# A graph attention layer whose steps leave their per-product queues for one timetable over three groups

## The chip, the cores and the metric

The kernel runs on one core of a Trainium2 chip. The metric is device time in microseconds (us) of one execution. The times given are medians of several runs; the profile is of one further execution, whose span is given beside them. Engine names are those of the profile: PE (matmul) with PEld (its weight loads), DVE, ACT, POOL, and SP, which issues the DMAs.

## What is computed

The input `x` has 128 graphs of 128 nodes with 768 features; `adj` has one 128 x 128 matrix per graph. There are 12 heads of 64 features.

```python
h = jnp.maximum(_layernorm(x, axis=-1), 0.0)
q, k, v = (_split_heads(h @ W + b) for W, b in ((Wq, bq), (Wk, bk), (Wv, bv)))
scores = jnp.einsum('bhqd,bhkd->bhqk', q, k) / jnp.sqrt(HD) + beta * adj[:, None]
scores = jnp.where(adj[:, None] > 0, scores, -9e15)
out = jnp.einsum('bhqk,bhkd->bhqd', softmax(scores), v)
x = x + out.transpose(0, 2, 1, 3).reshape(B, N, D)
```

All is in float32.

## The kernel before

**Groups and slices.** Four graphs make a group; there are 32 groups, 0 to 31. For each group three slices of the projections are computed: `qk0` (Q and K of heads 0 to 5), `v`, and `qk1` (Q and K of heads 6 to 11). Group 0 does them by ordinary blocked matmuls (`plain_slice`, L834); in that stage the weights' blocks are also prepared. Groups 1 to 31 do each slice as a fast matrix multiplication, 15 block products instead of the ordinary count (`PRODUCTS`, L66): each product multiplies one sum of activation blocks (`S..`, or a block `A..` itself) by one prepared sum of weight blocks (`T..`). So a group has 45 products, and this document numbers them as slots 0 to 44: 0 to 14 `qk0`, 15 to 29 `v`, 30 to 44 `qk1`. A product is itself made of seven zones (L556), each two matmuls of 128 rows, 64 stationary columns and 128 moving columns (L561); a float32 matmul leaves two records, so a product leaves 28.

**Chains and PSUM.** The fifteen products belong to four chains, a to d (third entry of a row in `PRODUCTS`). A chain adds up in one pair of PSUM banks; four such pairs exist (L160), handed out in turn (`take`, `give`). After each product the chain's running sum is evicted into the Q, K or V block that uses it (L567 to L585): the first time into a fresh "home" by ACT (the opening, L579 and L581; for V by DVE and ACT, L575 and L576), later by DVE, which adds or subtracts (L585). The chain's next product can start only when the eviction has read the bank. A pair is also taken by each step of scores (L631) and by each attend (L687), so these share the four pairs with the chains. Homes are seven plus one added after group 0 (L527, L1076), handed out in turn too.

**Blocks that are streamed.** Of the 45 weight blocks 11 are resident (`RESIDENT`, L116, by their place in the sequence of a group); the other 34, of 448 KB each, are loaded for each group into a ring of five buffers (`load_T`, L336). A load is issued on SP right behind the product that frees the buffer.

**The other steps of a group.** When the last eviction of a home is done, it is decoded on POOL, sometimes on DVE (L595): four or five elementwise operations that undo the zones. Scores of a pair of heads follow (L640), then the mask on DVE (L648), which writes e and frees the pair, and exp on ACT (L650). An attend is woven into the matmuls of one product (`turn`, L522); ACT then takes the result from the bank (the drain, L707 and L709), DVE makes reciprocals (L668), ACT divides (L680), DVE adds x (L725), and SP sends the result (L728). For the next group x is loaded (L191), normalized on ACT (L452), transposed by DVE (L473), completed by POOL (`inner`, L483 to L485), and summed by DVE into the `S` blocks (L478). For the group after that, rows of x are loaded (L415) and their sums and sums of squares taken on ACT (L423 to L425). The bias of a group is loaded from adj on SP (L492), transposed by DVE (L501), squared in place on ACT (L502), masked and added up by DVE (L504, L506).

**What sets the order.** The program is written in the order in which each engine executes it, each engine's queue being in order. `run` (L822) issues the matmuls of a product, then `behind_product` (L812): masks waiting, then the steps that a table gives for this slot (`todo`, filled from L1082 on), then drains, then steps put off by a count of slots (`later`, L512); then the product's evictions, then `trail` (exp, divide), then the slot's "post" steps. So an eviction always stands behind its slot's sums and transposes, and decodes, divisions and additions come a fixed number of slots behind what they follow. The order of the products within a slice is given by hand (L109 to L114).

Of the kernel before, what the change touches and what calls it, by code (L numbers as in the profile page):

```python
# [10 lines left out]
F32 = mybir.dt.float32  # L11
# [97 lines left out]
ZORDER = (1, 0, 3, 5, 2, 7, 10, 6, 11, 13, 4, 9, 14, 8, 12)  # L109
QORDER = (4, 0, 1, 8, 2, 3, 5, 6, 7, 10, 9, 11, 13, 12, 14)  # L110
LORDER = (1, 4, 0, 8, 5, 2, 10, 3, 6, 7, 13, 9, 11, 12, 14)
# [8 lines left out]
LAG = {("v", 8): 4, ("v", 12): 4, ("qk1", 11): 4}  # L120
ZONES = (5, 1, 2, 3, 4, 0, 6)
LEFT = (6, 2, 1, 4, 3, 5, 0)
# [5 lines left out]
def direct(ctx, tc, x, adj, wq, bq, wk, bk, wv, bv, beta, out, bad):  # L128
# [141 lines left out]
    def prepare(sl):  # L270

        def home(name):
            n = [i for i, p in enumerate(PRODUCTS) if p[1] == name][0]
            if (sl, n) in resident:
                return resident[sl, n]
            made_in[0] += sl != "qk1"
            if sl != "qk1" and made_in[0] % 8 in (2, 5, 7):
                t = work.tile([P, 2, W], F32, tag="e", name=f"prep_{sl}_{n}", bufs=3)
                return t.rearrange("p i w -> p (i w)")[:, 0:7 * P].rearrange("p (z n) -> p z n", n=P)
            return work.tile([P, 7, P], F32, tag="T", name=f"prep_{sl}_{n}", bufs=RING)  # L280
# [46 lines left out]
    def order_of(G, sl):  # L327
        if G == 1 and sl == "qk0":
            return ZORDER
        return LORDER if G == NG - 1 and sl == "qk1" else ORDER[sl]  # L330
# [22 lines left out]
    bqk = const.tile([P, 3, NC], F32, name="bqk")  # L353
# [51 lines left out]
    rows = {}  # L405
# [21 lines left out]
    def row_moments(G, first=5, then=8):  # L427

        ve = stat.tile([P, GRP], F32, tag="verow", name=f"verow_{G}", bufs=1)
        nc.vector.tensor_scalar(ve, rows[G][:, 2], 1.0 / D, EPS, op0=ALU.mult, op1=ALU.add)  # L430
        mean = rows[G][:, 1]
        t = stat.tile([P, 2, GRP], F32, tag="row2", name=f"row2_{G}", bufs=1)

        def powers():
            nc.gpsimd.tensor_tensor(t[:, 0], ve, nhalf.to_broadcast([P, GRP]), ALU.pow)
            nc.gpsimd.tensor_tensor(t[:, 1], mean, t[:, 0], ALU.mult)

        later(powers, 2)
        to = stat.tile([P, NB, 2, GRP], F32, tag="block2", name=f"block2_{G}", bufs=1)
        turned = dram.tile([SQ, NB, 2 * GRP], F32, name=f"turned_{G}")  # L440
        later(lambda: nc.sync.dma_start(turned.rearrange("i b s -> b i s"), t.rearrange("p s g -> p (s g)")), first)
        later(lambda: nc.sync.dma_start(to.rearrange("p b s g -> p (b s g)"),
                                        turned.rearrange("i b s -> i (b s)")[None].to_broadcast([NB, SQ, NB * 2 * GRP])), then)
        for g in range(GRP):
            for b in range(NB):
                rstd[G, g * NB + b], shift[G, g * NB + b] = to[:, b, 0, g:g + 1], to[:, b, 1, g:g + 1]

# [14 lines left out]
    def home_A(G, name):  # L462
        if (G, name) in wide:
            return A[G, name]
        t = wide[G, name] = work.tile([P, 2 * GRP, P], F32, tag=name, name=f"{name}_{G}", bufs=1 + (name[1] == "0"))
        full[G, name] = t[:, 0:7]
        A[G, name] = t[:, GRP:2 * GRP].rearrange("p (c g) n -> p c (g n)", c=2)
# [12 lines left out]
    def inner(G, name):  # L480
        t = wide[G, name]
        e = nc.gpsimd
        e.tensor_tensor(t[:, 0:2], t[:, 7:8].to_broadcast([P, 2, P]), t[:, 5:7], ALU.subtract)  # L483
        e.tensor_tensor(t[:, 2], t[:, 6], t[:, 0], ALU.subtract)
        e.tensor_tensor(t[:, 3], t[:, 4], t[:, 2], ALU.subtract)  # L485
# [9 lines left out]
    turned = {}  # L495

    def bias_steps(G):

        raw = turned.pop((G, "raw")).rearrange("p g b j -> p g (b j)")
        t = biasT[G] = work.tile([P, GRP, N], F32, tag="biasT", name=f"biasT_{G}", bufs=2)  # L500
        nc.vector.transpose(t, raw)  # L501
        trailing.append(lambda: nc.scalar.activation(raw, raw, AF.Square, scale=beta_s, accum_out=seen[:, NG + G:NG + G + 1]))  # L502
        yield
        nc.vector.tensor_scalar(raw, t, 0.0, MASKED, op0=ALU.is_le, op1=ALU.mult)  # L504
        yield
        nc.vector.scalar_tensor_tensor(t, t, beta_c, raw, op0=ALU.mult, op1=ALU.add)  # L506
# [20 lines left out]
    homes = deque(const.tile([P, 7, P], F32, name=f"home{i}") for i in range(7))  # L527
# [17 lines left out]
    def product_z(G, sl, n):  # L545
# [6 lines left out]
        p = banks[chain].rearrange("p i (z w) -> p (i z) w", w=P)  # L552
# [13 lines left out]
        yield  # L566
        for (r, j), sign in uses:  # L567
            key = (G, sl, r, j)
            op = ALU.add if sign > 0 else ALU.subtract
            if key not in qk:  # L570
                left[key] = sum(k == (r, j) for q in PRODUCTS for k, _ in q[3])
                t = qk[key] = home_qk(*key, zones=True)
                if sl == "v":
                    bias = bv_b[:, j * 2 * P:(j + 1) * 2 * P].rearrange("p (i n) -> p i n", i=2)
                    nc.vector.tensor_tensor(t[:, 5:7], bias, p[:, 5:7], op)  # L575
                    nc.scalar.activation(t[:, 0:5], p[:, 0:5], AF.Copy, scale=float(sign))  # L576
                else:
                    oc = j + 3 * int(sl[2])
                    nc.scalar.activation(t[:, 0:5], p[:, 0:5], AF.Copy, scale=float(sign))  # L579
                    for at, of in ((5, 0), (6, 2)):  # L580
                        nc.scalar.activation(t[:, at], p[:, at], AF.Identity, bias=bqk[:, of, oc:oc + 1],  # L581
                                             scale=float(sign))
            else:
                t = qk[key]
                nc.vector.tensor_tensor(t, t, p[:, 0:7], op)  # L585
            left[key] -= 1
            if not left[key]:
                last = order_of(G, sl) is LORDER
# [704 lines left out]
```

## Time and profile before

| | |
|---|---|
| median of 3 runs | 2685.24 us (2683.63 to 2687.36) |
| span of the profiled execution | 2683.5 us |
| busy: PE, PEld, DVE, POOL, ACT | 2654.5, 2564.6, 2179.1, 2073.5, 1750.2 us |
| group 0 (span's start to 124.2) | 124.2 us |
| group 1 | 83.9 us |
| groups 2 to 30 | 2371.7 us |
| group 31 to its last product's end | 88.5 us |
| end behind the last product | 15.2 us |
| DMA | 721.71 MB, mean 269 GB/s |

A row of a timeline gives the start, the time taken, the engine, the line, the operation, and output and input tiles with the count; what stands in brackets is the idle time before it and what ended it. A row of waits gives engine, tile and line that waited, and for what, then the total in us, how often, and the longest. A row of the windows gives a stretch, its length, the busy time and the count of each of PE, PEld, DVE, ACT and POOL, then the granted clock of PE, the DMA engines' share, and GB/s. Matmuls overlap, so a matmul's own time is longer than its distance to the next; distances from start to start tell PE's pace.

### The profile page before, as it was taken

The page shows a single profiled execution, that of the slowest core. Times are in us where ns is not written, and L with a number is a line of the kernel's source. Part 1 is how long each engine was busy: PE and PEld are TensorE (multiplying, and loading weights), DVE is VectorE, ACT ScalarE, POOL GpSimd, SP SyncE. Part 2 cuts the span into 40 slices and gives each one's busy share as a digit, 9 for nine tenths or more (in the row PEclk, how much of TensorE's full clock was granted, in tenths as well). Part 3 has the DMA queues.
Part 4 walks back from the last instruction along what each step waited for, and adds up shares of the span by engine and source line. Part 5 has one row for each costly group of instructions (what it writes and reads, how often), then busy time and mean ns, then how long its engine had stood idle before and what let it go on. Part 6 is the DMA issues. An engine that isn't in the chain of part 4 may idle for free.

```text
span 2683.5 us, 121478 instructions
## 1 busy us (share of the span) xinstructions
PE 2654.5 (99%) x52029; PEld 2564.6 (96%) x52029; DVE 2179.1 (81%) x2701; ACT 1750.2 (65%) x4608; POOL 2073.5 (77%) x3043
## 2 busy tenths in 40 slices
PE   9999999999999999999999999999999999999998
PEld 7799999999999999999999999999999999999997
DVE  6878888878888788888788877788877888877885
ACT  1567766676666677666766666776667676667654
POOL 5877778877778777788777787777887777877774
PEclk9999999999999999999999999999999999999999
DMA  9889888989889898889899889988898998898875
GB/s 232 286 253 281 280 270 274 280 264 284 275 267 279 262 285 270 273 276 279 265 281 279 270 269 278 279 274 276 269 278 265 274 284 270 272 274 274 258 239 162
DMA packets 530341, 721.71 MB, mean 269 GB/s; under 512 B 105980, under 2 KB 374024, under 8 KB 529800
## 3 DMA queue, kind: packets, MB, share of 16 engines
q1 hardware_dynamic: 528640, 713.12, 86.5%
q8 instruction: 411, 6.73, 1.0%
q10 hardware_dynamic: 1160, 0.79, 0.2%
q14 instruction: 130, 1.06, 0.1%
HBM read 647.73 MB, written 66.05 MB: 266 GB/s over the span
## 4 chain that ended last, share of the span: by engine, by line
PE 48%; POOL 27%; ACT 12%; issue 5%; DMA 5%; DVE 3%; SPq 1%; ACTq 0%; POOLq 0%; DVEq 0%
PE pair L561 36%; PE pair L697 4%; POOL v L618 4%; PE pair L857 3%; PE pair L640 3%; POOL v L617 3%; POOL home L616 3%; POOL A L483 3%; ACT x L452 3%; ACT e L650 2%; POOL home L603 2%; POOL home L605 2%; ACT home L579 2%; ACT home L581 2%; POOL v L614 2%
## 5 line engine op out<-in xcount | busy, mean ns | idle before, releaser
L585 DVE TENSOR_TENSOR home<-home,pair 128x896 f32<-128x896 f32 x810 | 861.1, 1076 | 276.2 <-PE pair L561 223.8
L561 PE MATMUL pair<-sbig,T_qk 128*64 128x128 f32 x13020 | 832.8, 273 | 2.9 <-DMA T_qk<-kept_qk 2.0
L561 PEld LDWEIGHTS pair<-sbig,T_qk 128*64 128x64 f32 x13020 | 707.8, 137 | 12.7 <-issue 6.9
L561 PE MATMUL pair<-A,T_qk 128*64 128x128 f32 x6944 | 465.3, 273 | 0.4 <-ACT e L709 0.4
L680 ACT ACTIVATE e<-e,sm 128x64 f32<-128x64 f32 x1512 | 383.0, 348 | 109.2 <-DVE sm L668 109.2
L603 POOL TENSOR_TENSOR home<-home 128x256 f32<-128x256 f32 x298 | 246.6, 828 | 267.8 <-DVE home L585 260.1
L561 PE MATMUL pair<-T_v,sbig 128*64 128x128 f32 x6944 | 417.4, 274 | 1.5 <-issue 1.5
L697 PE MATMUL pair<-v,e 128*64 128x65 f32 x6048 | 400.8, 221 | 5.6 <-DVE e L648 5.5
L579 ACT ACTIVATE home<-pair 128x640 f32<-128x640 f32 x325 | 231.7, 713 | 261.4 <-PE pair L561 200.9
L561 PEld LDWEIGHTS pair<-T_v,sbig 128*64 128x64 f32 x6944 | 381.5, 137 | 14.9 <-issue 13.1
L561 PEld LDWEIGHTS pair<-A,T_qk 128*64 128x64 f32 x6944 | 376.9, 137 | 5.4 <-ACT e L709 5.0
L697 PEld LDWEIGHTS pair<-v,e 128*64 128x64 f32 x6048 | 355.5, 137 | 15.6 <-DVE e L648 12.6
L561 PE MATMUL pair<-sbig,res_qk 128*64 128x128 f32 x4340 | 288.3, 273 | 0.0
L606 POOL TENSOR_TENSOR home<-home 128x256 f32<-128x256 f32 x298 | 239.7, 804 | 23.4
L604 POOL TENSOR_TENSOR home<-home 128x256 f32<-128x256 f32 x298 | 229.8, 771 | 23.4
L561 PEld LDWEIGHTS pair<-sbig,res_qk 128*64 128x64 f32 x4340 | 234.5, 137 | 5.3 <-issue 5.3
L707 ACT ACTIVATE sm<-pair,tiny 128x8 f32<-128x8 f32 x189 | 49.6, 262 | 283.2 <-PE pair L697 283.1
L452 ACT ACTIVATE x<-x,block 128x192 f32<-128x192 f32 x480 | 232.9, 557 | 0.0
L605 POOL TENSOR_TENSOR home<-home 128x128 f32<-128x128 f32 x298 | 212.6, 713 | 23.4
L648 DVE SCALAR_TENSOR_TENSOR e<-pair,biasT 128x1024 f32<-128x1024 f32 x189 | 225.1, 1217 | 4.7 <-PE pair L640 4.7
L650 ACT ACTIVATE e<-e 128x1024 f32<-128x1024 f32 x189 | 193.8, 1065 | 49.3 <-DVE e L648 46.1
L483 POOL TENSOR_TENSOR A<-A 128x256 f32<-128x256 f32 x186 | 168.6, 906 | 56.5 <-DVE A L473 56.5
(201 smaller groups left out, 4602.4 us busy)
## 6 DMA issues: line engine op xcount, KB each, us to landing
T_qk<-kept_qk SPq DMA_DIRECT2D x713, 448.0 KB, 4.9
T_v<-kept_v SPq DMA_DIRECT2D x341, 448.0 KB, 4.7
xo<-in_x_dram SPq DMA_DIRECT2D x189, 256.0 KB, 4.2
out_dram<-xo SPq DMA_DIRECT2D x189, 256.0 KB, 5.9
x<-in_x_dram SPq DMA_DIRECT2D x248, 192.0 KB, 6.8
sbig<-in_x_dram SPq DMA_DIRECT2D x116, 384.0 KB, 6.2
kept_qk<-prep_qk SPq DMA_DIRECT2D x23, 448.0 KB, 3.0
adj<-in_adj_dram SPq DMA_DIRECT2D x128, 64.0 KB, 3.9
```

Of the source, the lines that this page charges most:

```text
L452: nc.scalar.activation(t, t, AF.Relu, bias=shift[G, n], scale=rstd[G, n])
L483: e.tensor_tensor(t[:, 0:2], t[:, 7:8].to_broadcast([P, 2, P]), t[:, 5:7], ALU.subtract)
L561: nc.tensor.matmul(p[q:q + HD, at, :], lhs[:, q:q + HD], rhs, start=(first and at % 4 == 0), stop=True, skip_group_check=True)
L579: nc.scalar.activation(t[:, 0:5], p[:, 0:5], AF.Copy, scale=float(sign))
L585: nc.vector.tensor_tensor(t, t, p[:, 0:7], op)
L603: e.tensor_tensor(t[:, 1:4:2], t[:, 1:4:2], twice(5), ALU.add)
L604: e.tensor_tensor(t[:, 2:5:2], t[:, 2:5:2], twice(1), ALU.add)
L605: e.tensor_tensor(t[:, 4], t[:, 4], t[:, 6], ALU.add)
L606: e.tensor_tensor(t[:, 0:7:6], t[:, 0:7:6], twice(2), ALU.add)
L650: trailing.append(lambda: nc.scalar.activation(e, e, AF.Exp, scale=1.0 / ISCALE))
L680: nc.scalar.activation(o[:, r, b, 0:HD], pa[:, r, b, 0:HD], AF.Copy, scale=t[:, 1, r, b:b + 1])
L697: nc.tensor.matmul(pa[q:q + HD, 2 * g + i, :], k[:, q:q + HD], vt[G, "v", r, h // 4][:, 4 * g + h % 4, :], start=True, stop=True, skip_gro ...
```

## The change

**Steps become single actions with a time of their own.** The eviction is split from the product; mask, exp, drain, reciprocals, division, addition, sending, and the parts of the bias and of the row moments are functions that can be placed one by one. Each gets a time in slots (45 to a group) from a table: `TABLE` has one group's steps over three groups' time (from -97, two groups ahead, to 66), `EVICT` and `DECODE` give the distance behind the product, and the engine of a decode (p for POOL, v for DVE). Behind the matmuls of a slot all steps that are due before the next slot are issued in order of their times. Group 1 has its own entries for the steps of group 0 (`FIRST`, `SECOND`), and its own evictions and decodes (`first`); the last group has its own (`LAST`, `vlast`, `last`). The halves of masks and the split opening that the code now knows are not used (`OPEN` is empty).

**Other product orders**, for the three slices in general, for the first slice of group 1, and for two slices of the last group. **Other resident blocks**, again 11. **Buffers**: eight homes plus the one added after group 0; the tiles of the `A` blocks have seven 128-wide parts instead of eight, and the order of the parts changes with that.

```diff
-ORDER = {"qk0": XORDER, "v": PORDER, "qk1": QORDER}
+ORDER = {"qk0": (1, 0, 5, 2, 10, 3, 6, 7, 13, 11, 9, 4, 14, 12, 8), "v": (1, 0, 5, 2, 10, 3, 6, 7, 13, 11, 4, 9, 14, 8, 12), "qk1": (4, 1, 0, 8, 2, 5, 3, 6, 7, 10, 9, 11, 13, 12, 14)}
-RESIDENT = (3, 8, 12, 16, 20, 25, 29, 33, 35, 38, 41)
+RESIDENT = (0, 2, 13, 19, 21, 26, 31, 33, 34, 36, 37)
+EB = 3
+HOMES = 8
...
+TABLE = (
...
+    (-18.549, 'adj'), (-18.495, 'inner', 'A11'), (-16.935, 'bias1'),
+    (-16.93, 'square'), (-15.753, 'bias2'), (-13.292, 'turn', 'A10'), (-12.008, 'inner', 'A10'),
+    (-9.066, 'bias3'), (-8.852, 'turn', 'A12'), (-8.634, 'sum', 'S1'), (-8.072, 'inner', 'A12'),
...
+    (45.566, 'send', 1), (45.956, 'divide', 0), (47.501, 'scores', 1, 2), (47.554, 'scores', 1, 0),
+    (47.953, 'mask', 3), (49.02, 'mask', 5), (50.562, 'exp', 5), (50.646, 'add', 0),
+    (51.524, 'scores', 1, 1), (51.602, 'mask', 4), (51.766, 'xo', 4), (51.972, 'send', 0),
+    (52.058, 'attend', 5), (52.932, 'exp', 3), (53.405, 'drain', 5), (53.474, 'xo', 3),
...
+DECODE = {
+    ('qk0', 1, 1): (2.293, 'p'), ('qk0', 1, 0): (3.04, 'p'), ('qk0', 0, 1): (1.026, 'p'), ('qk0', 1, 2): (4.055, 'p'),
...
+EVICT = {
+    ('qk1', 5, 0): 0.934, ('qk0', 14, 0): 0.762, ('v', 13, 0): 0.391, ('qk1', 4, 0): 0.124,
+    ('v', 3, 0): 0.85, ('qk0', 6, 0): 0.799, ('qk0', 11, 0): 0.955, ('qk1', 6, 0): 2.087,
...
+    def slice_z(G, sl, todo):
+        order = order_of(G, sl)
+        base = 45 * G + 15 * ("qk0", "v", "qk1").index(sl)
+        name = {(1, "qk0"): "first", (NG - 1, "v"): "vlast", (NG - 1, "qk1"): "last"}.get((G, sl), sl)
+        for k, n in enumerate(order):
+            outs = product(G, sl, n)
+            for i, f in enumerate(outs):
+                put(base + k + EVICT.get((name, n, i), 0.5), f)
...
+            behind_product(k, todo)
+            while events and events[0][0] < base + k + 1:
+                _, _, f, args = heapq.heappop(events)
+                f(*args)
             trail()
...
+    for G in range(NG):
+        for at, name, *args in TABLE if G else FIRST:
+            if 45 * G + at >= 45 and not (G == 1 and (name, *args) in SOONER) and not (
+                    G == NG - 1 and at >= 30 and not (name in ("mask", "exp") and args[0] < 3)):
+                put(45 * G + at, actions[name], G, *args)
...
     for G in range(1, NG):
-        more = G + 1 < NG
-        todo.clear()
-        then(2 + (G == 1), scores, G - 1, 1, 2)
...
+        for sl in ("qk0", "v", "qk1"):
+            if (G, sl) != (NG - 1, "qk1"):
+                slice_z(G, sl, todo)
```

Steps of the table as they fall into a group's slots, where the prediction names them: products 10, 3, 6 of `qk0` are in slots 4, 5, 6 (before 5, 4, 6); the opening of product 10 is due at 4.29, the adding eviction of product 6 at 6.80, the mask of the third scores (head pair 4) at 6.60, the attend of head pair 5 at 7.06 (so woven into slot 8, as before); row sums at 7.45, the opening of product 13 at 8.24, the drain of that attend at 8.41; chain d's first product of `qk0` is in slot 11 (before 10). The x loads are due at 12.48 and 37.23, the adj loads at 26.45, the bias transpose at 28.07 and its square at 28.07 (before: slots 26 and 30), the openings of product 4 in `qk1` at 30.12 and 30.71, for slot 33. Scores of head pairs 1 and 2 stay in slot 17.

More of the change, by code (lines that the diff above doesn't have):

```diff
@@ L1 @@
+import heapq
 import math
@@ L565, in product_z @@
             load_T()
[L566 to L575, printed above, removed]
-                    nc.scalar.activation(t[:, 0:5], p[:, 0:5], AF.Copy, scale=float(sign))
+        done = [len(uses)]
@@ L586, in product_z @@
[L586 to L593 removed]
+        left[key] -= 1
     def decode(G, sl, r, j, e=nc.gpsimd):
         t = qk[G, sl, r, j]
+        assert not left[G, sl, r, j]
```

417 lines of the change are left out of this document (260 added, 157 removed), and 21 rows, old and new, of tables (DECODE, EVICT, TABLE).

## The prediction

> **What bounds the kernel now.** I read the page first (shares), then windows cut at the starts of the groups, then the timeline of the matmul engine, then the list of waits of PE and of its weight loads (PEld). Slot k is the k-th of a group's 45 products.
>
> ```profile
> span 2683.5 us, 121478 instructions
> PE 2654.5 (99%) x52029; PEld 2564.6 (96%) x52029; DVE 2179.1 (81%) x2701; ACT 1750.2 (65%) x4608; POOL 2073.5 (77%) x3043
> ```
> ```profile
> 124.20:208.10 83.90, 81.86 (x1646) 79.59 (x1644) 67.64 (x81) 58.97 (x160) 62.01 (x89) 1.00 0.87 268
> 208.10:2579.80 2371.70, 2361.80 (x47680) 2303.95 (x47678) 1947.91 (x2292) 1600.56 (x4214) 1872.34 (x2726) 1.00 0.89 273
> ```
> PE sets the time. The second window holds groups 2 to 30: 2371.7 / 29 = 81.78 us each, at full clock. What could a group take? The timeline shows what PE needs where nothing holds it:
>
> ```profile
> 1185.67 0.39 PE L561 MATMUL pair<-A,T_qk 128*64 128x128 f32 x4
> ...
> 1188.13 6.35 PE L561 MATMUL pair<-sbig,T_qk 128*64 128x128 f32 x112
> 1194.41 1.98 PE L640 MATMUL pair<-home 64*64 64x128 f32 x64
> 1196.31 1.75 PE L561 MATMUL pair<-sbig,res_qk 128*64 128x128 f32 x28
> 1197.89 3.23 PE L561 MATMUL pair<-sbig,T_qk 128*64 128x128 f32 x56
> 1200.95 1.70 PE L561 MATMUL pair<-A,T_qk 128*64 128x128 f32 x28
> ...
> 1203.61 1.75 PE L561 MATMUL pair<-sbig,T_qk 128*64 128x128 f32 x28
> ```
> 28 records are a product. From start to start a plain product takes 1.53 us (two from 1197.89 to 1200.95), one with an attend woven in 2.46 (1185.67 to 1188.13), one with scores behind it 2.66 (1200.95 to 1203.61), the product after scores 1.58 (1196.31 to 1197.89), one with two scores behind it 3.59 (8.18 for four products, less three plain ones). A group has 31 plain ones, 6 with an attend, 2 with scores, 4 after scores and 2 with two scores: 47.4 + 14.8 + 5.3 + 6.3 + 7.2 = **81.0 us**. So 0.78 us per group, 22.6 in all, is waiting. The list of waits (groups 2 to 30; us in total, times, longest) names most of it:
>
> ```profile
> PEld pair L697 <- DVE e L648: 12.6, 29, 0.5
> PEld pair L561 <- ACT e L709: 5.0, 28, 0.4
> PEld pair L561 <- ACT home L581: 2.5, 5, 1.0
> PE pair L561 <- DMA T_qk<-kept_qk: 2.0, 4, 0.8
> ```
> The first two recur in nearly every group. By the Trainium skill (Perfetto Trace Analysis, Identifying the Most-Contended Engine) matmul busy time says little on headroom, and LDWEIGHTS busy time is the measure. Here PEld's 96% would leave 4%, about 119 us; the starts above show 1%, and I go by them.
>
> **The change, part by part.** It adds no product and no transfer: 34 of 45 blocks are streamed per group as before, 448 KB each. It moves steps within the queues of DVE, ACT, POOL and SP. What counts is who stands before whom at the waits above.
>
> *Slot 8, first attend.* Before, the third mask frees the pair that the attend takes, and it stands behind an eviction that itself waits for ACT:
>
> ```profile
> 1285.07 1.09 DVE L585 TENSOR_TENSOR home<-home,pair 128x896 f32<-128x896 f32 x1 [0.80 <-ACT home L581]
> 1286.07 1.22 DVE L648 SCALAR_TENSOR_TENSOR e<-pair,biasT 128x1024 f32<-128x1024 f32 x1
> ```
> After, product 10 runs in slot 4 instead of 5, so its opening is done earlier, and the mask (6.60) stands ahead of product 6's eviction (6.80). Counted from slot 0, product 5's slot ends at 11.3; DVE then does product 3's eviction (1.00 from start to start), an output addition (0.68, a row below), a sum (1.09, taken like the eviction of the same width) and the mask (1.22): done at 15.3. The attend's first matmul is due at 15.5 and a seventh of a product, 15.7. Slack 0.4; the 12.6 us go.
>
> *Slot 10, new bank.* Before, ACT does the row sums of squares (2.12 us) ahead of the drain that frees the pair:
>
> ```profile
> 1274.09 2.02 ACT L680 ACTIVATE e<-e,sm 128x64 f32<-128x64 f32 x8
> 1276.01 0.69 ACT L579 ACTIVATE home<-pair 128x640 f32<-128x640 f32 x1
> 1276.59 0.62 ACT L581 ACTIVATE home<-pair,bqk 128x128 f32<-128x128 f32 x2
> 1277.09 0.99 ACT L452 ACTIVATE x<-x,block 128x192 f32<-128x192 f32 x2
> ...
> 1287.38 1.06 ACT L650 ACTIVATE e<-e 128x1024 f32<-128x1024 f32 x1 [1.48 <-DVE e L648]
> 1288.35 0.83 ACT L423 ACTIVATE sbig<-sbig 128x768 f32<-128x768 f32 x1
> ...
> 1290.47 0.25 ACT L707 ACTIVATE sm<-pair,tiny 128x8 f32<-128x8 f32 x1
> 1290.62 0.58 ACT L709 COPY e<-pair 128x520 f32<-128x520 f32 x1
> ```
> These rows give ACT's prices: division 1.92, opening 1.08, exp 0.97, drain 0.63. After, chain d starts in slot 11 (at 22.0), and the drain, behind row sums, norm, exp and an opening, is done near 19.8. The 5.0 go.
>
> *Evictions late on ACT (2.5).* The worst order after is slots 0 to 3: opening (done 2.7; slot 2 needs it at 3.05), division (4.6), opening (5.7; slot 3 needs it at 6.6, since two scores lie between). They hold by 0.35 and 0.9, so I take the 2.5 off.
>
> *SP and the streams (2.0).* A block has to be there when its product starts:
>
> ```profile
> T_qk<-kept_qk SPq DMA_DIRECT2D x713, 448.0 KB, 4.9
> ```
> ```profile
> 766.77 3.15 SPq L191 DMA_DIRECT2D x<-in_x_dram  x4
> ...
> 777.38 1.27 SPq L341 DMA_DIRECT2D T_qk<-kept_qk  x2
> ```
> Before, the four x loads of slot 36 hold SP for 3.15 us, a row load behind them waits, and two blocks wait behind that. After, the x loads come at 37.23, with products 36 and 37 resident (no block is issued there). With five buffers a block has at least four products, 6.1 us, and a score or attend besides, 7 us or more, against 4.9. The price of ten streamed slots in a row (3 to 12) and seven (38 to 44) shows nowhere: between 0 and 1 us a group, nearest to 0 by that slack. I take the 2.0 off.
>
> *POOL's decodes for the scores of slot 17.*
>
> ```profile
> 1298.53 0.73 POOL L603 TENSOR_TENSOR home<-home 128x256 f32<-128x256 f32 x1
> ...
> 1301.38 0.73 POOL L603 TENSOR_TENSOR home<-home 128x256 f32<-128x256 f32 x1
> 1302.20 1.12 POOL L604 TENSOR_TENSOR home<-home 128x256 f32<-128x256 f32 x1
> ```
> ```profile
> 1302.04 0.68 DVE L725 TENSOR_TENSOR xo<-xo,e 128x512 f32<-128x512 f32 x1
> ```
> A decode takes 2.85 us, and 0.4 more beside an output addition. After, two decodes start when slot 12's eviction is done (27.4) with two additions beside them: 27.4 + 5.7 + 0.8 = 33.9, due at 34.6. Slack 0.7. The Trainium skill (SBUF — State Buffer, Who interferes with whom) speaks against this: a DVE instruction with two SBUF inputs and a GpSimd one that reads SBUF exclude each other, and the loser waits fully. By that each addition could cost 0.68, the slack is nearly used, and the sum would stand up to 0.1 us per group, 3 us, higher; the row shows 0.4, so I stay with it.
>
> *The ninth buffer* only takes away waits of ACT for a free home, none of them PE's; narrower A tiles cost nothing, since no instruction grows.
>
> *What it adds.* A chain's next product must wait until the chain's previous product is evicted. Pairs of products of one chain only two slots apart were 6 per group and become 12. An opening (1.08) must fit into the one product between (1.53): 0.45 to spare if ACT is free, and an exp ahead (0.97) would lose 0.5. No row of before has these pairs; bounds 0 and 0.5 us each. By the sums above and the same for slots 17, 24 and 38 (0.45 to 0.5 spare) they are nearer to 0; I allow 0.1 us per group, 2.9.
>
> *First and last group.* Group 1 takes 83.9, 2.1 over the mean of the others, and its longest wait on PE is at its scores in slot 17:
>
> ```profile
> PE pair L640 <- issue: 1.4, 1, 1.4
> ```
> Its product order and score slots change, so I take this 1.4 off, between 0 and -2.4. In the last group scores of half a pair move behind the last product (a mask and an exp of half the width, 0.6 and 0.5, with their matmuls and waits up to 2.5), and a decode leaves DVE for POOL (up to 2.85, its time there): between -3 and +2.5, I take 0.
>
> **Sum**: 2683.5 - 12.6 - 5.0 - 2.5 - 2.0 + 2.9 - 1.4 = 2662.9 for the profiled execution. The median of the runs (2685.24) lies 1.7 above that execution's span, so **2664.6 us**.
>
> **Rivals.** *A, queues a little late*: orders are right, but sums of DVE beside POOL run longer and half the gain stays. For it: many slacks of 0.35 to 0.7. Against: DVE is busy 67 of 81.8 us, so lateness is made up soon. Losing 0.3 us per group gives 2664.6 + 8.7 = 2673.
>
> *B, the bias after its load*: the bias transpose moves from slot 30 to slot 28, two products nearer to the adj loads of slot 26.
>
> ```profile
> DMA to landing us min/median/max: 3.4/3.9/5.5
> ```
> Issued from 49.3 on for some 2 us, the last lands near 55.1, when DVE is ready for it (54.9). The square on ACT stands ahead of product 4's two openings, which slot 33 needs at 59.9. At 3.9 nothing is lost; at 5.5 in every group 0.6 us, 17 us: 2682, no change to speak of.
>
> *C, slower*: the six new tight pairs each lose. The place is slots 2 to 4 and 5 to 9, ACT and DVE; it decides from 0.15 us per pair (6 x 29 x 0.15 = 26 us, the 20.6 gained and 0.2%). At 0.2 us it gives 2664.6 + 34.8 = 2699. For it: 12 pairs instead of 6. Against: the six of before cause no wait on an adding eviction in PE's list.
>
> *D, better*: all 22.6 go and no wait comes, group 1 loses its 2.4 and the end 3: 2683.5 - 28.0 + 1.7 = 2657.
>
> **How the numbers follow.** Forecast (2660 to 2670) 0.60, A 0.15, B 0.06, C 0.11, D 0.08. A measurement of this kernel can tell about 0.2% (5.4 us) from no change. Faster is forecast, A and D: 0.83; same is B: 0.06; slower is C: 0.11. The range, 2656 to 2681, reaches from just below D to just below B and holds forecast, A and D, 0.83; B and C are left out.
>
> **What would show it.** The wait of L697 for the mask and that of the products for the drain vanish from PEld's list; groups 2 to 30 take about 81.1 us each. Wrong it is if PE waits for evictions (A, C: home or pair written by ACT or DVE in slots 2 to 9), for openings in slot 33 (B), or if blocks land late in slots 8 to 15 or 43 to 1.

## The result, and the profile after

The kernel after takes **2699.95 us** (median of 4 runs, 2698.23 to 2703.59) against 2684.8 in 4 runs of the kernel before on the same chip: ratio 1.0058, 95% interval 1.0043 to 1.0072. It is slower by 0.6%, where 0.8% faster was forecast. The profiled execution took 2698.23 us, its span 2696.3.

Where the time went is read first from windows cut at the starts of the groups (start:end, length, then busy time of PE, PEld, DVE, ACT, POOL, clock, DMA share, GB/s):

```profile
0.00:124.98 124.98, 118.74 (x872) 93.92 (x872) 92.58 (x214) 39.76 (x90) 81.98 (x149) 0.99 0.84 241
124.98:210.46 85.48, 82.38 (x1644) 79.64 (x1646) 68.90 (x86) 60.30 (x164) 62.28 (x92) 1.00 0.89 283
210.46:2597.50 2387.04, 2360.85 (x47680) 2307.34 (x47678) 1896.25 (x2291) 1612.31 (x4214) 1855.55 (x2725) 1.00 0.87 271
2597.50:2680.60 83.10, 83.10 (x1712) 81.16 (x1708) 61.41 (x88) 44.48 (x124) 45.28 (x64) 1.00 0.72 224
```

Before and after: group 0 124.2 and 125.0, group 1 83.9 and 85.5, groups 2 to 30 2371.7 and 2387.0, group 31 88.5 and 83.1, the end 15.2 and 15.7. So 15.3 us were lost in the groups that were forecast to gain 19.2, and the last group gave 5.4 back.

The waits of PE and its weight loads in groups 2 to 30 (engine and line, for whom, us in total, times, longest):

```profile
PEld pair L778 <- issue: 24.3, 106, 1.3
PEld pair L683 <- issue: 24.2, 120, 1.7
PEld pair L683 <- ACT home L728: 13.6, 17, 1.4
PEld pair L683 <- ACT sbig L728: 5.3, 6, 1.6
```
```profile
PE pair L683 <- ACT home L728: 9.2, 13, 1.2
PE pair L778 <- issue: 7.5, 11, 1.3
```
The waits for the mask and for the drain, which the prediction took away, are gone. In their place stand the openings of a Q or K block (L728) and "issue" at the scores (L778), an idle time for which the trace names nobody.

**Loss of a slot**, below, is its length (from start to start of the products) less the third shortest of the 29, summed over groups 2 to 30; a wait that comes in every group is not seen by it. The shortest lengths add up to 80.92 us a group; the floor of 81.0 that the prediction put together was right. By this count slots 32 and 33 lose 18.5 us after and nothing before, slots 17 and 18 lose 16.4 after and 2.4 before, and all other slots together 5.4.

**First place: slots 32 and 33.** The timelines of DVE, ACT and PE in group 3 after (start, time, engine, line; in brackets the idle time and what ended it):

```profile
351.21 0.71 DVE L607 STREAM_TRANSPOSE biasT<-adj 128x512 f32<-128x512 f32 x1 [1.97 <-DMA adj<-in_adj_dram]
```
```profile
351.96 0.72 ACT L611 ACTIVATE adj<-adj,beta_s 128x512 f32<-128x512 f32 x1 [2.62 <-DVE biasT L607]
...
352.68 0.68 ACT L726 ACTIVATE sbig<-pair 128x640 f32<-128x640 f32 x1
353.26 0.61 ACT L728 ACTIVATE sbig<-pair,bqk 128x128 f32<-128x128 f32 x2
353.76 0.71 ACT L726 ACTIVATE home<-pair 128x640 f32<-128x640 f32 x1
354.34 0.64 ACT L728 ACTIVATE home<-pair,bqk 128x128 f32<-128x128 f32 x2
```
```profile
352.52 1.70 PE L683 MATMUL pair<-sbig,T_qk 128*64 128x128 f32 x28
355.04 0.44 PE L683 MATMUL pair<-A,res_qk 128*64 128x128 f32 x4 [0.82 <-ACT home L728]
```
DVE stands idle until adj has landed, ACT stands idle until the transpose is done, and behind ACT's square wait the two openings that slot 33 needs. From the transpose's start to PE's restart it is 3.83 us. Rival B of the prediction is this chain.

**Second place: the scores of slot 17.** PE in group 3:

```profile
326.38 1.53 PE L778 MATMUL pair<-home 64*64 64x128 f32 x47
329.25 0.27 PE L778 MATMUL pair<-home 64*64 64x128 f32 x1 [1.34 <-issue]
329.26 0.70 PE L778 MATMUL pair<-sbig 64*64 64x128 f32 x16
```
PE stops within a run of matmuls of one step. The list puts the weight load's part of this wait down to POOL's decode:

```profile
PEld pair L778 <- POOL home L744: 4.3, 17, 1.6
```
Sixteen of these 17 are 0.17 us long, and there the weight load goes on within 0.2 us of the decode's end. The seventeenth is this one, 1.58 us, and the decode had ended 0.38 us before PE went on. The matmul just ahead of that weight load waited for nothing that the trace names and stood nearly as long. So it is not the decode. The page's list of DMA queues has one that moves instructions:

```profile
q8 instruction: 412, 6.75, 1.0%
```
Its 412 packets are of 16384 bytes. The trace has 105,265 instructions of PE (matmuls, weight loads, and 1,207 of its sequencer), 255.5 to a packet, and 13 packets to a group. By the Trainium skill (Runtime: NRT & Kernel Launch, Instruction fetch mechanics) an engine's instructions come in blocks of 256 by a DMA queue of its own, at a cost that is "mostly hidden". The counts agree; hidden it is not here: in group 3 a packet passes from 326.84 to 327.88, and PE goes on 1.37 us after it. A group has 3326 such instructions, 2 fewer than 13 blocks, so a block ends at nearly the same place in every group, and one of the 13 ends in or behind the two score steps of slot 17. Before, a group has 3324, and that end moves further: from slot 17 in group 2 to slot 19 in group 30, where after it reaches slot 18. The place alone doesn't make the loss: in groups 2 to 10, where it differs by less than 0.4 us, slots 17 and 18 lose 0.7 us before and 7.9 after.

**Theories before the experiments.** For slot 32: the bias is placed too near its load. Rival: ACT's queue is late anyway. For slot 17: instruction packets come late because the DMA engines are full there. Rivals: the place of the block's end alone; the speed of the scores (64 instructions in a little over 1 us, where a product has 56 in 1.53); a wait for data that the trace doesn't name.

### The profile page after: what moved, and what is told of

It reads as the page before. It is cut to its first block, busy times and chain, and to the rows that moved or that the text cites. A ratio compares the mean times of both kernels' runs of the same rounds, so it can differ in the third digit from the quotient of the medians.

```text
span 2696.3 us, 121389 instructions
## 1 busy us (share of the span) xinstructions
PE 2650.7 (98%) x52029; PEld 2566.0 (95%) x52029; DVE 2129.9 (79%) x2712; ACT 1762.1 (65%) x4608; POOL 2049.4 (76%) x3033
## 4 chain that ended last, share of the span: by engine, by line
PE 85%; DMA 4%; ACT 2%; SPq 2%; DVE 1%; issue 1%; POOL 1%; DVEq 0%; POOLq 0%; ACTq 0%
PE pair L683 72%; PE pair L778 7%; PE pair L857 6%; DMA adj<-in_adj_dram 4%; SPq L601 2%; ACT home L726 1%; ACT home L728 1%; DVE biasT L607 1%; PE pair L1054 0%; SPq L440 0%; DMA sbig<-in_L_gnn_Wk_dram 0%; ACT sbig L726 0%; DVE sbig L587 0%; ACT sbig L728 0%; ACT adj L611 0%
## 5 line engine op out<-in xcount | busy, mean ns | idle before, releaser
L706 DVE TENSOR_TENSOR home<-home,pair 128x896 f32<-128x896 f32 x836 | 890.2, 1077 | 263.2 <-PE pair L683 173.5
L741 POOL TENSOR_TENSOR home<-home 128x256 f32<-128x256 f32 x300 | 268.6, 895 | 300.0 <-DVE home L706 299.7
L683 PE MATMUL pair<-T_v,sbig 128*64 128x128 f32 x6944 | 411.0, 274 | 3.4 <-issue 2.6
L683 PEld LDWEIGHTS pair<-T_v,sbig 128*64 128x64 f32 x6944 | 382.4, 137 | 15.7 <-issue 14.2
L683 PE MATMUL pair<-A,T_qk 128*64 128x128 f32 x6076 | 394.8, 273 | 0.9 <-DMA T_qk<-kept_qk 0.7
L683 PEld LDWEIGHTS pair<-A,T_qk 128*64 128x64 f32 x6076 | 334.0, 137 | 2.4 <-DMA T_qk<-kept_qk 1.4
L683 PE MATMUL pair<-sbig,res_qk 128*64 128x128 f32 x4340 | 266.0, 273 | 0.9 <-DVE home L706 0.9
L742 POOL TENSOR_TENSOR home<-home 128x256 f32<-128x256 f32 x300 | 242.1, 807 | 23.5
L744 POOL TENSOR_TENSOR home<-home 128x256 f32<-128x256 f32 x300 | 239.4, 798 | 23.5
L683 PE MATMUL pair<-A,res_qk 128*64 128x128 f32 x2604 | 206.1, 274 | 14.5 <-ACT home L728 9.2
L728 ACT ACTIVATE home<-pair,bqk 128x128 f32<-128x128 f32 x648 | 203.0, 373 | 0.0
```

The lines of the kernel that those rows point to most:

```text
L683: nc.tensor.matmul(p[q:q + HD, at, :], lhs[:, q:q + HD], rhs, start=(first and at % 4 == 0), stop=True, skip_group_check=True)
L741: e.tensor_tensor(t[:, 1:4:2], t[:, 1:4:2], twice(5), ALU.add)
L742: e.tensor_tensor(t[:, 2:5:2], t[:, 2:5:2], twice(1), ALU.add)
L744: e.tensor_tensor(t[:, 0:7:6], t[:, 0:7:6], twice(2), ALU.add)
```

## The experiments

Every median is set against the kernel before on the same chip; it took 2684 to 2687 us there.

**1. Bias later** (e1_bias_later).
```diff
-    (-16.935, 'bias1'), (-16.93, 'square'), (-15.753, 'bias2')
+    (-14.25, 'bias1'), (-14.24, 'square'), (-13.0, 'bias2')
```


> The changed kernel with one edit: in every group from the second on, the bias transpose and the square move from slot 28 to 30.75, behind product 4's two openings, and the mask of the bias from 29.2 to 32. Theory (the bias comes too soon after its load): the transpose no longer waits for the adj load, or waits with nothing urgent behind it; the 17.2 us that groups 2 to 30 lose between slots 32 and 33 go, and 2699.95 falls by 15 to 19 us, to about 2682. Rival (ScalarE's whole queue is late around slot 30, the square only happens to be in it): the openings stay late, the square now delays what is behind it, and the gain is under 6 us. Neither theory touches the waits at slots 17 and 18 (16.4 us), which should stay.

2679.1 us, ratio 0.9973 (0.9962 to 0.9984). Slots 32 and 33 lose 0.1 us, groups 2 to 30 take 2370.0, slots 17 and 18 lose 18.9. L728 has left the list; what is left on PE above 1 us is issue:

```profile
PE pair L683 <- issue: 7.2, 10, 1.8
PE pair L778 <- issue: 7.2, 10, 1.3
```
adj lands as late as before the edit (5.3 us in the median); nothing urgent waits for it.

**2. adj sooner** (e2_adj_earlier), the bias where the change has it.
```diff
-    (-18.549, 'adj')
+    (-22.6, 'adj')
```


> The changed kernel with one edit: the four adj loads of a group are issued at slot 22.4 in place of 26.45; the bias transpose stays at slot 28. Theory (the landing of adj is what is late): about 4 slots or 6.5 us more than cover a landing of 2.8 to 9.1 us, the DVE wait for adj (47.9 us in 30 groups) goes to under 5 us and the time falls by 14 to 19 us as with the later bias. Rival 1 (the order on ScalarE is what is late, not adj): under 4 us of gain. Rival 2 (the DMA engines are so full that moving 256 KB earlier only delays the streamed block behind it): the gain is eaten by waits for blocks in slots 22 to 27, which show as PE waiting for T_v.

2686.03 us, ratio 0.9993 (0.9984 to 1.0003). The last adj packet now passes 0.2 us after the start of slot 26 in place of 7.0, DVE's wait for adj is gone and so is the loss at slot 32: ACT's queue as such was not late. But slot 29 now loses 4.9 us to late blocks of `qk1` (PEld waits 5.3 us for T_qk, 7 times) and slot 41 5.8 to issue: rival 2 is right that the traffic moved hits something else, though not the V blocks it named.

**3. The old resident blocks** (e3_resident_before).
```diff
-RESIDENT = (0, 2, 13, 19, 21, 26, 31, 33, 34, 36, 37)
+RESIDENT = (3, 8, 12, 16, 20, 25, 29, 33, 35, 38, 41)
```


> The changed kernel with one edit: the 11 resident blocks stand in the slots where the old kernel had them (3, 8, 12, 16, 20, 25, 29, 33, 35, 38, 41), so that no run of streamed blocks is longer than 4; all orders and tables stay. Theory (uneven residents load the DMA engines unevenly, and both late adj loads and late instruction fetches come from that): the adj landing's maximum falls from 9.1 to about 6, the loss at slot 32 from 17.2 to under 6 us, the loss at slots 17 and 18 from 16.4 to under 6, and the time falls by 15 to 28 us. Rival (places alone: the bias too near its load, the code block's end in the double scores): both losses stay within 4 us of what they are, and the time within 0.2%.

2737.02 us, ratio 1.0198 (1.018 to 1.0217). Both losses stay (slots 17 and 18 17.8, slot 32 22.3), and slots 44, 1 and 2 lose 29.2 us to late blocks and to issue. The theory that uneven residents make both losses falls. The median landing of one adj load is back at 4.0 us here (3.9 before the change), and slot 32 loses all the same.

**4. Code shifted by half a block** (e4_code_half_block): behind the warming matmuls stands
```diff
+    for n in range(32):
+        nc.tensor.matmul(warm[:, 0, 0:8], ident, ident[:, 0:8], start=True, stop=True)
```


> The changed kernel with 32 small extra matmuls (8 columns each) behind the 13 warming ones, so that TensorE's instruction stream after them lies half a 16 KB packet of the instruction queue (128 of 256 instructions) further on; they write a bank that is opened anew afterwards. They cost group 0 some 2 to 6 us, read off the start of group 1. Theory (TensorE waits at the two scores of slot 17 for its next instruction packet, whose boundary falls there): the issue waits at slots 17 and 18 (16.4 us) go to under 6 us, perhaps with a few at another slot, and groups 2 to 30 get 8 to 15 us shorter. Rival (it is a wait for data that the trace doesn't name, as the decode of the keys on GpSimd or a bank): slot 17 and 18 keep their 16 us within 3. Slot 32 keeps its 17 us under both.

2706.15 us, ratio 1.007 (1.0057 to 1.0083). Group 0 takes 10 us longer, where 2 to 6 were expected, and slot 32 loses 23.4 us, where 17 were. Slots 17 and 18 fall from 16.4 to 2.5, but slots 19 to 21 now lose 12.9. PE in group 3 of this kernel:

```profile
341.69 1.25 PE L683 MATMUL pair<-res_v,sbig 128*64 128x128 f32 x19
343.21 0.76 PE L683 MATMUL pair<-res_v,sbig 128*64 128x128 f32 x9 [0.27 <-issue]
```
It stops between matmuls 19 and 20 of a product whose operands and bank are all there. The wait goes where the code goes, so it is for instructions and not for data. It is not the scores' speed alone either: slots 19 and 20 have no scores. In total the loss is hardly smaller, which the theory had not expected. The traces bear the theory out further. Count PE's instructions in order, a weight load ahead of its matmul: in groups 2 to 30 of all 16 kernels there are 125 issue waits that put two matmuls 0.7 us or more apart, and all of them end at number 193 or 194 of a run of 256 (counted from 0), in whatever slot that falls. So that is where the trace's blocks end.

**5 and 6. Less traffic** (e5_sends_later, e6_no_row2), both on top of the later bias.
```diff
-    (58.233, 'send', 5), (63.766, 'send', 4), (66.076, 'send', 3)
+    (67.0, 'send', 5), (67.6, 'send', 4), (68.2, 'send', 3)
```


> The kernel with the later bias (2679.1 us, 18.9 us of its waits at slots 17 and 18) with one more edit: the three stores of 256 KB that it issues at slots 13.2, 18.8 and 21.1 are issued at 22.0, 22.6 and 23.2, where the DMA engines are less busy. Theory (TensorE's instruction packets come late at slots 17 and 18 because the DMA engines are full there): 768 KB less in slots 13 to 21 start the packet of slot 17 some instructions earlier, the waits at 17 and 18 fall from 18.9 to under 8 us and the time to 2665 to 2671; the adj load of slot 26.45 may land later, behind which nothing urgent waits now. Rival (the packet is late for another reason, its place in the program alone, or reads matter and stores don't): 17 and 18 stay at 15 to 22 us and the time within 4 us of 2679.

2698.3 us, ratio 1.0048 (1.0036 to 1.006). Slots 17 and 18 lose 22.0, and slot 29 a further 13.3 to late blocks; adj lands after 6.9 us in place of 5.3.

```diff
     def load_row(G, g):
+        if G > 2 and g == 2:
+            return
```


> The kernel with the later bias, leaving out one load: from group 3 on the row of sample 2 (384 KB, issued at slot 15.9) is not loaded, and its statistics are taken of the row that stands there, so part of the result is of other data. Theory (full DMA engines make the instruction packet late): 384 KB less just ahead of the packet of slot 17 take most of the 18.9 us at slots 17 and 18 away, to under 6 us, and the time falls to 2662 to 2668. Rival (place in the program alone): 17 and 18 stay at 15 to 22 us, the time within 4 us of 2679.

2682.47 us, ratio 0.9987 (0.9977 to 0.9998); slots 17 and 18 lose 23.5. The theory falls in this form: less traffic in these slots does not take the loss away. The second run, which leaves out a load, was a poor test too: the row is issued only 2.0 us after the start of slot 17, and its 3072-byte packets pass 3.7 to 6.8 us after it, behind the instruction packet.

**7. The two scores apart** (e7_scores_apart), on top of the later bias.
```diff
-    (17.953, 'scores', 0, 2)
+    (18.06, 'scores', 0, 2)
```


> The kernel with the later bias with one more edit: of the two score blocks of slot 17 the second comes one product later, in slot 18; loads and stores stay. Rival theory (the late packet only costs because two score blocks in a row use up instructions twice as fast as products do): the instructions ahead of the packet last longer by about half a score block's worth, and the waits of slots 17 to 19 fall from 18.9 to under 8 us, the time to 2666 to 2672. Theory (the packet is late by the DMA load wherever it falls in slots 13 to 21): the waits stay at 13 to 20 us, spread over 17 to 19, and the time within 5 us of 2679.

2679.57 us, ratio 0.9985 (0.9975 to 0.9994). The waits fall from 18.9 to 6.8 us, as the rival said, but the time does not: with scores behind two products in place of one the shortest lengths add up to 81.23 in place of 80.88 us, 10 us over 29 groups. So the speed of the scores sets what a late packet costs, not that it is late.

**8. The old kernel with the bias sooner** (e8_before_bias_sooner).
```diff
             turn_act(G + 1, ((10, "A11"),), 1)
+            bias(G + 1, 13)
...
-        bias(G + 1, 0, 2, 4)
+        bias(G + 1, 0, 4)
```


> The old kernel with one edit: the bias transpose and square move from slot 30 to 28 and the mask of the bias from 32 to 30, as in the changed kernel; the adj load stays at slot 26, residents and orders stay. Theory (the place alone makes the loss, also with the old landing of 3.4 to 5.5 us): the openings of slots 30 to 32 wait behind the square and the time grows by 10 to 20 us over the old kernel's. Rival (the place was harmless at the old landing times and only the later landing of the new order of transfers, 5.2 in the median and up to 9.1 us, makes the loss, as the price put on it in the prediction assumes): the time stays within 5 us of the old kernel's.

2694.3 us, ratio 1.0034 (1.0021 to 1.0047), between the two expectations. Slots 31 to 33 lose 8.5 us, and group 1 takes 2.3 longer. The place alone makes about half of the loss; the other half goes with adj's last packet, which passes 7.0 us after the start of slot 26 in the changed kernel (8.5 at most) and 6.5 here (7.5 at most).

**A new theory.** Listing the packets by size shows a load whose time near slot 17 differs: the second half of x (768 KB in packets of 768 bytes) passes from 5.2 us ahead of the start of slot 17 to 0.4 ahead before, and from 2.7 ahead to 2.1 behind after. The instruction packet has to pass in that time. (Of these packets the middle 96% are taken here and below.)

**9 and 11. The x load sooner** (e9_x_sooner on top of the later bias, e11_after_x_sooner alone).
```diff
-    (-32.522, 'load_x', 1)
+    (-35.0, 'load_x', 1)
```


> The kernel with the later bias (2679.1 us) with one more edit: the load of the second half of the inputs (768 KB in packets of 768 bytes, which pass in slots 15 to 17) is issued at slot 10.0 in place of 12.5, so that its packets should pass in slots 13 to 15, as they do in the old kernel. Theory (TensorE's instruction packet starts late while these packets pass, about 1.2 to 3 us after the start of slot 17, and the two score blocks use up what is left): the packet starts before 1.2 us in most groups, the waits of slots 17 and 18 fall from 18.9 to under 6 us, and the time to 2663 to 2669. Rival (the place of the packet's boundary in the program alone, or the burst of streamed blocks in slot 17): the waits stay at 13 to 22 us and the time within 5 us of 2679.

> The changed kernel with the input load at slot 10.0 alone, the bias left where the change put it. Theory (two causes that add): the 16.4 us at slots 17 and 18 go to under 6, the 17.2 us at slot 32 stay within 4, and the time falls from 2699.95 by 9 to 15 us, to 2685 to 2691. Rival (both are one late train of transfers, so that an earlier input load also lets adj land earlier): slot 32 falls under 10 us too, and the time to 2675 to 2683.

2689.36 us (1.0025, 1.0012 to 1.0038) and 2711.89 us (1.0117, 1.0096 to 1.0138): slower. Slots 17 and 18 fall to 4.3 and 6.1 us, where under 6 was expected, but slot 16 now loses 18.7 and 19.4, and the waits of the first of these kernels say why:

```profile
PE pair L683 <- DMA T_v<-kept_v: 14.7, 19, 2.1
```
768 KB put ahead of a streamed block make the block late. This wait also makes up most of the fall at slots 17 and 18, for PE stands 0.65 us a group in slot 16 and the packet uses that time. Counted from the start of slot 16, which the wait does not move, the packet starts at 2.7 and 2.6 us, and at 3.0 and 2.8 in the kernels without this edit. So a sooner x load hardly brings the packet sooner. Slots 32 and 33 lose 18.2 us in the second: that loss does not hang on the x load.

**10. The old kernel with the x load later** (e10_before_x_later).
```diff
-            then((12, "post"), load_x, G + 1, 1)
+            then((14, "post"), load_x, G + 1, 1)
```


> The old kernel with one edit: the load of the second half of the inputs is issued two slots later, behind slot 14 in place of 12; it is needed by the normalisations that run from slot 21 on. Theory (the 768-byte packets make the instruction packet of slot 17 late): they pass in slots 15 to 18, the waits at slots 17 to 19, 3.6 us now, grow to 10 to 22 us, and the time rises by 7 to 18 us over the old kernel's. Rival: the waits stay under 7 us and the time within 4 us.

2680.56 us, ratio 0.9986 (0.9977 to 0.9995): the opposite. The packets of x now pass behind the start of slot 17 (1.4 to 5.4 us), and the instruction packet goes ahead of them, 1.1 us before that start. Slots 17 to 19 lose 0.9 us in place of 3.6.

**12 and 13. The changed kernel with the x load later**, with the later bias (e12_x_later_bias_later) and without (e13_after_x_later).
```diff
-    (-32.522, 'load_x', 1), (-26.732, 'norm', 3, 0, 2), (-26.487, 'norm', 2, 0, 2)
+    (-30.4, 'load_x', 1), (-24.4, 'norm', 3, 0, 2), (-24.3, 'norm', 2, 0, 2)
```


> The kernel with the later bias (2679.1 us, 18.9 us lost at slots 17 and 18) with the input load two slots later, at 14.6, and the first two normalisations of that half at slots 20.6 and 20.7 in place of 18.3 and 18.5. Theory (the instruction packet of slot 17 is held up only by the 768-byte packets that pass at that time; behind it they do no harm): the packet starts before the start of slot 17 in nearly all groups, slots 17 and 18 lose under 4 us, groups 2 to 30 take 2353 to 2358 us and the whole 2661 to 2668, below both kernels. Rival (the later load makes ScalarE's normalisations, and the openings and transposes behind them, late): a new loss of 8 us or more in slots 19 to 26.

> The changed kernel with the later input load and the two later normalisations alone, the bias left where the change put it. Theory (two causes that add): the loss at slots 17 and 18 falls from 16.4 to under 4 us, that at slot 32 stays at 14 to 20 or grows by what the later train of transfers adds to the landing of adj, and the time is 2681 to 2690. Rival (one late train of transfers behind both): slot 32 moves as much as slot 17 does, up if adj lands later by over 1.5 us in the median, and the time stays at 2695 or more.

2673.81 us (0.9959, 0.9945 to 0.9972) and 2691.63 us (1.003, 1.0019 to 1.0041). Slots 17 and 18 lose nothing in either; slots 32 and 33 keep 12.9 us in the second, somewhat less than the 14 expected, and its time is 1.6 us above the range. The time of the first is 5 us or more above what was expected, for a reason that its waits name:

```profile
PEld pair L683 <- ACT home L718: 8.1, 18, 0.5
PEld pair L683 <- ACT sbig L718: 2.9, 6, 0.5
```
An opening of a V block (L718), 9.3 us at slot 24. What the x load does is seen over ten of the kernels (medians of groups 2 to 29, in us from the start of slot 17; then the time to the instruction packet's start from the end of the block before, where PE takes the last number 193; the loss is that of groups 2 to 30):

```
kernel                     x packets pass   packet starts   after block's end   loss at 17, 18
before                     -5.2 to -0.4      1.1             2.7                 2.4
after                      -2.7 to  2.1      1.3             3.5                16.4
later bias                 -2.7 to  2.1      1.5             3.6                18.9
old residents              -4.5 to  1.0      1.6             3.8                17.8
later bias, sends later    -2.7 to  2.4      0.9             3.2                22.0
later bias, x sooner       -7.6 to -2.7      0.5             3.5                 4.3
x sooner                   -7.7 to -2.7      0.4             3.2                 6.1
before, x later             1.4 to  5.4     -1.1             1.0                 0.2
later bias, x later         0.0 to  5.0     -1.3             1.1                 0.0
x later                     0.1 to  5.1     -1.2             1.1                 0.0
```
The time from the block before decides, not where x passes. Left aside are run 4, whose blocks end elsewhere, run 7, whose block lasts longer, and runs 9 and 11, where PE also waits for a V block. Over the 12 other kernels the groups in which the packet starts up to 3.0 us after the block before lose 2.6 us in slots 15 to 19 in all, and the 146 others 123.8. A block takes 5.3 to 5.5 us undisturbed, the packet 1.0 to 1.3, and PE goes on 1.2 us or more after it, so by estimate about 3 us are free. In every kernel with x later, the packet starts 1.0 to 1.1 us after the block before; with x sooner it does not.

**14. One normalisation behind the opening** (e14_norm_behind_opening), on top of 12.
```diff
-    (-22.154, 'norm', 2, 2, 4)
+    (-21.55, 'norm', 2, 2, 4)
```


> The kernel with the later bias and the later input load (2673.81 us, profiled 2674.03) with one more edit: the last of the four normalisations of the second half moves from slot 22.85 to 23.45, behind the opening of the V product of slot 23. Theory (the 9.3 us lost at slot 24 are the order on ScalarE: one normalisation of about 0.44 us a step too much ahead of that opening): slot 24 loses under 2 us, the transpose of A11 comes about 0.5 us later with VectorE's slack to cover it, and the time falls to 2663 to 2668. Rival (the evictions and transposes behind it are late in turn): the loss moves to slots 25 to 29 and the time stays within 3 us of 2674.

2664.4 us, ratio 0.9922 (0.9908 to 0.9935), faster than both kernels. Groups 2 to 30:

```profile
208.92:2566.38 2357.46, 2352.53 (x47681) 2306.08 (x47679) 1900.59 (x2290) 1612.13 (x4214) 1853.18 (x2725) 1.00 0.89 275
```
That is 81.29 us a group; slot 24 loses nothing.

## Why the prediction was wrong, by its steps

**The floor, slot 8, slot 10, late evictions: right.** Without slots 17, 18, 32 and 33 the groups 2 to 30 after would take 2387.0 - 16.4 - 18.5 = 2352.1, 19.6 less than before; the terms for these groups (-12.6 - 5.0 - 2.5 - 2.0 + 2.9) came to 19.2. With the two causes undone, run 14 ends at 2664.4, where 2664.6 was forecast; that closeness owes something to chance, since the last group's gain and group 1's loss were not in the sum.

**Rival B: the mechanism right, the price wrong.** It was given 0.06 and "nothing is lost" at a landing of 3.9 us. Two sizes failed. The four loads of adj were taken to issue in "some 2 us"; SP needs 3.0 in the median after (2.6 before), here 3.10:

```profile
343.93 3.10 SPq L601 DMA_DIRECT2D adj<-in_adj_dram  x4
```
And the median landing of one load was put behind the issue, where the transpose waits for the last packet of four. The prediction put that at 55.1, 5.9 us after the start of slot 26 (49.2); the trace of before itself has it at 6.8. With 3.83 us from the transpose's start to PE, and slot 33 due 10.7 us after slot 26, the transpose must start within 6.87 us. Its median after is 7.44, and 23 of the 29 groups lose, up to 1.5 us each. By the prediction's own numbers there was 1.0 us of slack; in the median 0.6 us were missing.

**SP and the streams: the step that failed most.** The price of the long runs of streamed slots was put "between 0 and 1 us a group, nearest to 0", and taken as 0. The streamed blocks did arrive in time, so as a wait for blocks the term was right. But other transfers in the same queue moved with them. V blocks land after 6.3 us in the median where it was 4.7 (the tile T_v before, then after):

```profile
DMA to landing us min/median/max: 3.1/4.7/8.7
DMA to landing us min/median/max: 3.4/6.3/9.4
```
And the x load, though placed half a slot sooner, passes 2.5 us later. SP already issues it 1.6 us later in the median, 2.2 us after the start of slot 12 in place of 0.6, because a row's load and the block's load behind slot 12's product, which is streamed now, stand ahead of it. Group 3 before and after, where slot 12 starts at 313.84 and 316.17:

```profile
314.40 2.60 SPq L191 DMA_DIRECT2D x<-in_x_dram  x4
```
```profile
316.80 0.49 SPq L515 DMA_DIRECT2D sbig<-in_x_dram  x1
317.91 0.32 SPq L440 DMA_DIRECT2D T_v<-kept_v  x1
318.32 2.14 SPq L288 DMA_DIRECT2D x<-in_x_dram  x4
```
This is what brought it onto the instruction packet, which starts 3.5 us after the block before in place of 2.7. Run 3 warns against taking x alone for the cause: there it passes 1.1 to 1.7 us sooner than after the change, and the loss stays. The 14.0 us more that slots 17 and 18 lose, 0.5 us a group, would fit the bound of the term; but a wait for instructions was not what it priced. That a late instruction packet has a price stood in no term, though before's page had the queue and its list of waits an issue of 1.4 us at the scores of slot 17 in group 1, which the prediction hoped to lose with the new order of the products. In the trace of before an instruction packet passes just ahead of that wait's end too.

**Rival C: not what happened.** The tight pairs of products cost next to nothing; the waits for evictions in slots 2 to 9 that it named did not come. It was slower for another cause.

**POOL's decodes, the ninth buffer: no cost seen.** Slots 17 and 18 lose nothing once the packet is in time, so the slack of 0.7 held where it was put.

**First and last group.** Group 1 took 1.6 us longer, where 1.4 less was forecast: its wait at the scores of slot 17 shrank only by 0.6 us, its first slice took 0.8 longer, and slots 32 and 33 lost 1.4. The last group won 5.4, beyond the bound of 3. No run took this apart; from the starts of its products, slots 39 to 43 take 9.8 us in place of 15.0.

**What stays open.** That the last wait is for an instruction packet, and that an x load issued later frees it, is shown. Why the packet is held up otherwise isn't settled. The size of the x load's packets alone is not the reason: in run 9, between the end of the block before and the packet, 29 KB of 768-byte packets pass on average and 967 KB of blocks and rows, and after the change 607 KB of the x load and 158 KB of blocks. How much of the 14 us between before and after the x load makes, and how much the other transfers, no run tells. By the Trainium skill (DMA: Bandwidth & Descriptors, Queues, rings and completion order) a DMA engine changes between queues only behind a whole packet of a queue; no run here shows whether that is the reason.

## What to carry to other kernels

When a change shifts the order of transfers, price every transfer in the queue, and above all who waits for the last packet of a group of loads, not the median of one. Instructions are a transfer as well: find where the code's blocks end, and see that the packet isn't held up just then, in particular ahead of steps that use up instructions fast; here a long load issued later, behind the packet, did it, and the same load issued sooner did not. A step moved nearer to its load must be checked against what stands behind its consumer on each in-order engine; here a square that nobody was in a hurry for held up two openings.

## What the runs showed of the hardware

- In the changed kernel PE lost 0.1 to 1.8 us at a block's end near slot 17 in 20 of 29 groups, and went on 1.2 to 1.6 us after the instruction packet had passed. Nearly all of this loss, in 12 kernels, fell in groups where the packet started more than 3.0 us after the end of the block before.
- A 768 KB load issued some two slots later brought the start of the instruction packet forward by 2.2 to 2.8 us, counted from the start of slot 17. Issued 2.5 slots sooner, it brought it forward by 0.2 to 0.3 us, counted from the start of slot 16.
- Four adj loads of 64 KB in 128-byte pieces hold SP for 3.0 us in the median (1.9 to 4.0).
- Scores behind two neighbouring products cost 0.35 us a group more than two scores behind one product.
